# Head of a graph-transformer block: x in smaller pieces on two queues, edge lists cast by ScalarE, rows and columns in another order

## The chip, the cores and the metric

The kernel runs on one core of a Trainium2 chip. Its time is the device time of one execution in microseconds; the figure used is the median of several runs. A core has five engines that work side by side, each on its own list of instructions: TensorE (PE, with its weight loads PEld), VectorE (DVE), ScalarE (ACT), GpSimd (POOL) and SyncE (SP, which only issues transfers and synchronises). Transfers are issued from the queues of SP, ScalarE and GpSimd; the engine that issues one spends a few tenths of a microsecond on it and goes on. An engine takes its instructions in order: where one waits, all behind it wait.

## The reference, cut to what matters

The inputs are x (625 rows of 768), two lists of 20625 edge ends, src and dst (sorted by dst), and many weights. The whole is one layer of a graph transformer:

```python
xn = _layernorm(x, axis=-1)
x = x + gnn(xn, stack([src, dst]), ...) + mix(xn[None], ...)[0]
x = x + ffn(_layernorm(x, axis=-1)[None], ...)[0]
```

`gnn` is a first dense layer x1 = relu(xn @ W_ah + b_ah), three graph attentions over x1 with four heads each, and an output product. `mix` is a linear attention with a projection. `ffn` is a softmax attention, a normalisation over all elements, and a mixture of eight experts of which two are used. For the head of the kernel only this counts: xn is the normalised x; x1 is computed from xn; and the edges have to be turned into a 625 by 625 matrix of counts, how many edges go from each source to each target.

## The kernel before, in words

The 625 rows of x are five blocks of 125 rows, one row per partition. `xs` holds them. The head does the following.

- **Loads** (L141 to L162, an order written out by hand for SP and ScalarE): src goes out on ScalarE's queue and dst on SP's; then blocks 0 and 1 of x, by `load_x` and `move_rows` (L73): 112 rows in one transfer and the remaining 13 in a second. Block 0 is on SP, block 1 on ScalarE. Then SP issues the first half of W_ah (`wah0`, 1152 KB) and blocks 2 to 4; ScalarE issues `brow0`, the bias of the first dense layer. Outside that hand-written order, ScalarE has `fetch` (L189), a one-column copy ahead of which the activation table is loaded.
- **Are the edges near their place?** dst is sorted, so the target of edge number e is near a straight line. VectorE subtracts the line (L216), takes the absolute value (L217), the largest per partition (L219) and compares it with a bound (L220); a one-column matmul into the bank `psfar` adds the partitions up (L222), and `missed` (L224) becomes 0 or 1. All engines read `missed` at L262 and skip a slow path where it is 0.
- **Edge columns.** src and dst arrive as 55 partitions of 375. VectorE casts them from integer to float (`rf`, L226), TensorE transposes them, three pieces each, into the banks `ps_0` and `ps_1` (L231), and VectorE copies the banks to `src_f` and `dst_f` (L235), from which the 0/1 matrices for the counting products are made later (L249, L255).
- **First rows.** `row_stats` takes mean and variance of a block (two statistics instructions L88, one aggregation L90, an addition L92, all VectorE) and raises the variance to the power of minus one half on GpSimd (`rs`, L94). `norm_rows` writes the normalised block `xn` on VectorE (L207). `first_rows` (L319) transposes it on TensorE, four pieces into one bank and two into another (`ptx`, L323); ScalarE copies the banks to `xnT` (L324).
- **First products.** With `xnT` of blocks 0 and 1 TensorE begins x1 (`psx`, L357) in `x1_slice`; ScalarE applies bias and relu (L368).

The accumulator banks psfar, ps_0, ps_1, pb0 (the transposed bias, L497), ptx and psx are of one pool with four banks (`psb`, L109); one that its last reader has left goes to the next tile that asks.

Order of the work: in this part VectorE, TensorE and GpSimd follow the order of the program text (`manual_schedule` at L212, L213 and L495), ScalarE is in the text's order for the loads alone. What is not written out so is ordered by a planner, which puts instructions that it takes to be ready by their place in the text. Semaphores are inserted by the compiler.

Of the kernel before, what the change touches and what calls it, by code (L numbers as in the profile page):

```python
# [11 lines left out]
I32 = mybir.dt.int32  # L12
U32 = mybir.dt.uint32
AF = mybir.ActivationFunctionType
OP = mybir.AluOpType
# [7 lines left out]
TP = 125  # L23
# [16 lines left out]
def kernel(ctx: ExitStack, tc: tile.TileContext, a: dict, out: bass.AP):  # L40
    nc = tc.nc
# [31 lines left out]
    def move_rows(engine, dst, src):  # L73

        engine.dma_start(dst[0:112], src[0:112])
        engine.dma_start(dst[112:TP], src[112:TP])
# [7 lines left out]
    def row_stats(src, name):  # L84

        st = small.tile([TP, 2, 6], F32, tag="st", name=f"st_{name}")
        for j in range(2):
            nc.vector.bn_stats(st[:, j, :], src[:, j * HALF:(j + 1) * HALF])  # L88
        mv = small.tile([TP, 2], F32, tag="mv", name=f"mv_{name}")
        nc.vector.bn_aggr(mv, st.rearrange("p a b -> p (a b)"))  # L90
        ve = small.tile([TP, 1], F32, tag="ve", name=f"ve_{name}")
        nc.vector.tensor_scalar_add(ve, mv[:, 1:2], 1e-5)  # L92
        rs = small.tile([TP, 1], F32, tag="rs", name=f"rs_{name}")
        nc.gpsimd.tensor_tensor(rs, ve, mhalf[0:TP, 0:1], OP.pow)  # L94
        return mv, rs
# [16 lines left out]
    def b1(name):  # L112
        return psb.tile([P, BANK], F32, tag="b1", name=name)

    def mm(name):
        return psm.tile([P, 2 * BANK], F32, tag="mm", name=name)
# [6 lines left out]
    apool = es.enter_context(tc.tile_pool(name="apool", bufs=1, reuse_waits="tile"))  # L123
# [13 lines left out]
    NJ3 = NJ // 3  # L137
    SPREAD = 20
    idx_i = []
# [4 lines left out]
        eng.dma_start(idx_i[s], a[name].rearrange("(q e) -> q e", q=NJ3))  # L144
    xs = xpool.tile([TP, NT, D], F32, name="xs")
    def load_x(t):
        move_rows(nc.scalar if t == 1 else nc.sync, xs[:, t, :], a["x"][t * TP:(t + 1) * TP, :])

    wah = {}

# [3 lines left out]
    for t in range(2):  # L154
        load_x(t)
    load_ah(0)
    for t in range(2, NT):
        load_x(t)
# [26 lines left out]
    ones_col = const.tile([P, 1], F32, name="ones_col")  # L185
# [18 lines left out]
    def norm_rows(t, stats=None):  # L204
        mv, rs = stats or row_stats(xs[:, t, :], f"x{t}")
        xn = ohp.tile([TP, D], F32, tag="xn", name=f"xn{t}", bufs=3)
        nc.vector.tensor_scalar(xn, xs[:, t, :], mv[:, 0:1], rs, op0=OP.subtract, op1=OP.mult)  # L207
        return xn
# [4 lines left out]
    with tc.manual_schedule(engines={mybir.EngineType.DVE}):  # L213

        rf = [mxp.tile([P, N], F32, tag="kk", name=f"rf{s}", bufs=2)[0:NJ3, 0:3 * TP] for s in range(2)]
        nc.vector.scalar_tensor_tensor(odd, odd, -0.5 * PER, idx_i[1], op0=OP.mult, op1=OP.add)  # L216
        nc.vector.scalar_tensor_tensor(odd, odd, -1.0, odd, op0=OP.mult, op1=OP.max)  # L217
        far_s = small.tile([NJ3, 1], F32, tag="fs", name="far_s")
        nc.vector.tensor_reduce(far_s, odd, AX.X, OP.max)  # L219
        nc.vector.tensor_scalar(far_s, far_s, float(SPREAD), None, op0=OP.is_gt)  # L220
        ps = b1("psfar")
        nc.tensor.matmul(ps[0:1, 0:1], far_s, ones_col[0:NJ3], start=True, stop=True)  # L222
        missed = apool.tile([1, 1], I32, name="missed")
        nc.vector.tensor_scalar(missed, ps[0:1, 0:1], 1.0, None, op0=OP.min)  # L224
        for s in range(2):
            nc.vector.tensor_copy(rf[s], idx_i[s])  # L226
        ps = []
        for s in range(2):
            ps.append(b1(f"ps_{s}"))
            for r in range(3):  # L230
                nc.tensor.transpose(ps[s][0:TP, r * NJ3:(r + 1) * NJ3], rf[s][:, r * TP:(r + 1) * TP], ident[0:NJ3, 0:NJ3])  # L231
        st = [row_stats(xs[:, t, :], f"x{t}") for t in range(2)]
        xn = [norm_rows(0, st[0])]
        for s, f in enumerate((src_f, dst_f)):
            nc.vector.tensor_copy(f.rearrange("p (q r) -> p r q", r=3), ps[s][0:TP, 0:NJ].rearrange("p (r q) -> p r q", r=3))  # L235
        xn.append(norm_rows(1, st[1]))

        nc.vector.scalar_tensor_tensor(far, far, -PER, dst_f, op0=OP.mult, op1=OP.add)
        nc.vector.tensor_scalar(far, far, -0.5 * PER, None, op0=OP.add)
        nc.vector.scalar_tensor_tensor(far, far, -1.0, far, op0=OP.mult, op1=OP.max)  # L240
        nc.vector.tensor_scalar(far, far, float(SPREAD), None, op0=OP.is_gt)
        dst_all = apool.tile([TP, NJ], F32, name="dst_all")
        nc.vector.tensor_copy(dst_all, dst_f)
        nc.vector.scalar_tensor_tensor(dst_f, far, -2.0 * N, dst_f, op0=OP.mult, op1=OP.add)
        xn.append(norm_rows(2))
# [17 lines left out]
    with tc.If(again, preferred_fallthrough_block=True, label="far"):  # L263
        nc.vector.tensor_scalar(far, far, 2.0 * N, -2.0 * N, op0=OP.mult, op1=OP.add)
        nc.vector.tensor_add(far, far, dst_all)
        with tc.For_i(0, NJ, 1) as i:
# [4 lines left out]
            for b in range(NT):  # L271
                ps = mm(f"far{b}")
# [286 lines left out]
    for t in range(NT):  # L559
        nc.vector.tensor_sub(r12[:, t, 0, :], adn[:, t, :], mx[:, t, :])  # L560
        nc.vector.scalar_tensor_tensor(r12[:, t, 1, :], adn[:, t, :], 0.2, mx[:, t, :],
                                       op0=OP.mult, op1=OP.subtract)
# [143 lines left out]
    for g in range(2):  # L706
        w = load_w(rows(a["L0_mix_w_proj"], g * HALF, (g + 1) * HALF), f"wproj{g}")
        for t in range(NT):
            ps = b1(f"pspr{g}_{t}")
            for k in range(NC):  # L710
                nc.tensor.matmul(ps[0:TP, 0:HALF], yT[:, k, t * TP:(t + 1) * TP], w[:, k, :],  # L711
                                 start=(k == 0), stop=(k == NC - 1))
# [3 lines left out]
    ps = mm("psrT")  # L716
# [346 lines left out]
    ps = b1("psrs")  # L1063
# [45 lines left out]
    for hv in range(2):  # L1109
        lo, hi = HV[hv]  # L1110
        for c in range(NC):
            g, cc = divmod(c, 3)
            ps = b1(f"psw2{hv}{c}")
            for k in range(NC):
                nc.tensor.matmul(ps[:, 0:hi - lo], w2[g][:, k, cc * P:(cc + 1) * P], o2T[:, k, lo:hi],  # L1115
                                 start=(k == 0), stop=(k == NC - 1))
# [42 lines left out]
    for c in range(NC):  # L1159
        if c in (2, 5):  # L1160
            nc.scalar.activation(x3[:, c, 0:N], hT[:, c, :], AF.Identity, bias=gbi[:, c:c + 1], scale=gsc[:, c:c + 1])
        else:
            nc.vector.tensor_scalar(x3[:, c, 0:N], hT[:, c, :], gsc[:, c:c + 1], gbi[:, c:c + 1],
                                    op0=OP.mult, op1=OP.add)
# [139 lines left out]
    for k in range(2):  # L1304
        prw = a["L0_ffn_proj_w"][bass.ds(ex[k], 1), :, :].rearrange("e (f p) c -> p (e f) c", p=P)
        for u0 in range(0, HF, GU):
            hb = []
            for f in range(u0, u0 + GU):
# [11 lines left out]
                t = [ep.tile([P, NH2], F32, tag=f"t{q}", name=f"t{q}_{k}_{f}", bufs=GU + 2) for q in (1, 2, 4)]  # L1320
# [3 lines left out]
            for c in range(3):  # L1324
# [6 lines left out]
                for q in range(4):  # L1331
                    cc = c + 3 * (q // 2)
                    lo, hi = (0, NH2) if q % 2 == 0 else (NH2, N)
# [27 lines left out]
    def half(g):  # L1361
        return slice(g * HALF, (g + 1) * HALF)
# [23 lines left out]
    for i, (t, g) in enumerate(early):  # L1386
        if i == 0:
            nc.vector.scalar_tensor_tensor(xs[:, t, half(g)], ln2w[0:TP, half(g)], ngm[0:TP], xs[:, t, half(g)],
                                           op0=OP.mult, op1=OP.add)
# [7 lines left out]
    for i, at in enumerate([next(w) for w in (e, l, l, e, l, l, e, l, l, e)]):  # L1397
        t, g = at
        ps, dst = banks[at][0:TP, 0:HALF], fin[:, t, half(g)]
# [37 lines left out]
```

## Time and profile before

| what | value |
|---|---|
| median of 3 runs | 1338.31 us (1337.48 to 1338.95) |
| profiled execution | 1337.78 us |
| its span | 1336.0 us |
| TensorE clock granted | 0.997 of full |
| TensorE busy | 1305.2 us, 98% |
| VectorE busy | 794.2 us, 59% |
| ScalarE busy | 269.1 us, 20% |
| transfers | 109.00 MB, 82 GB/s on average |
| start of the first psx product | 13.28 us |

All times inside an execution are counted from the start of the span. In a line of the timeline the first number is the start, the second the duration in us, then engine, line, operation, output and inputs with their shapes; the bracket gives the engine's idle time before it and what ended it. An engine with a q behind its name is that engine's queue at work, such as issuing a transfer. In a line of the chain there are start, duration and what ran. In a line of waits there are the total in us, the number of times and the longest.

### The profile page before, as it was taken

The page shows a single profiled execution, that of the slowest core. Times are in us where ns is not written, and L with a number is a line of the kernel's source. Part 1 is how long each engine was busy: PE and PEld are TensorE (multiplying, and loading weights), DVE is VectorE, ACT ScalarE, POOL GpSimd, SP SyncE. Part 2 cuts the span into 40 slices and gives each one's busy share as a digit, 9 for nine tenths or more (in the row PEclk, how much of TensorE's full clock was granted, in tenths as well). Part 3 has the DMA queues.
Part 4 walks back from the last instruction along what each step waited for, and adds up shares of the span by engine and source line. Part 5 has one row for each costly group of instructions (what it writes and reads, how often), then busy time and mean ns, then how long its engine had stood idle before and what let it go on. Part 6 is the DMA issues. An engine that isn't in the chain of part 4 may idle for free.

```text
span 1336.0 us, 15063 instructions
## 1 busy us (share of the span) xinstructions
PE 1305.2 (98%) x5341; PEld 919.1 (69%) x5341; DVE 794.2 (59%) x2043; ACT 269.1 (20%) x550; POOL 79.5 (6%) x139
## 2 busy tenths in 40 slices
PE   7999999999999999999999969999999999999998
PEld 6676677556777895555667747777777777777776
DVE  7789687847575674675553386435543454445444
ACT  2122122014566570001011013101210021002100
POOL 3000111100000000000001130000000000000001
PEclk9999999999999999999999989999999999999999
DMA  8453232422212331103214132222212221322111
GB/s 242 130 149 89 75 102 73 145 86 74 73 63 69 107 103 35 36 26 105 71 36 139 36 110 67 62 74 83 72 56 82 83 71 49 86 80 72 48 48 58
DMA packets 124288, 109.00 MB, mean 82 GB/s; under 512 B 8990, under 2 KB 116470, under 8 KB 124212
## 3 DMA queue, kind: packets, MB, share of 16 engines
q1 hardware_dynamic: 114746, 84.79, 21.3%
q0 software_dynamic: 8464, 21.81, 5.2%
q10 hardware_dynamic: 1002, 1.43, 0.4%
q8 instruction: 42, 0.69, 0.2%
q14 instruction: 34, 0.28, 0.1%
HBM read 104.03 MB, written 3.96 MB: 81 GB/s over the span
## 4 chain that ended last, share of the span: by engine, by line
PE 89%; DVE 4%; issue 3%; ACT 2%; DMA 1%; POOL 0%; SPq 0%; DVEq 0%; ACTq 0%; POOLq 0%
PE psq L357 7%; PE ga_f L1206 6%; PE de_f L1206 6%; PE al_p L1206 6%; PE de_p L1206 6%; PE ga_p L1206 6%; PE al_f L1206 6%; PE psg L672 5%; PE cnt L257 3%; PE m_o L767 3%; PE be_f L1206 3%; PE pspr L711 3%; PE psw L1115 3%; PE be_p L1206 3%; PE psx L357 3%
## 5 line engine op out<-in xcount | busy, mean ns | idle before, releaser
L357 PE MATMUL psq<-xnT,wqkv 128*128 128x313 f32 (+1 forms) x432 | 121.8, 431 | 0.0
L672 PE MATMUL psg<-h,pt 125*125 125x193 f32 x600 | 101.2, 327 | 0.4 <-ACT node L677 0.4
L672 PEld LDWEIGHTS psg<-h,pt 125*125 125x125 f32 x600 | 98.5, 188 | 4.2 <-ACT node L677 0.7
L357 PEld LDWEIGHTS psq<-xnT,wqkv 128*128 128x128 f32 x432 | 78.9, 189 | 29.2
L1206 PE MATMUL al_f<-x,wf 128*128 128x313 f32 x288 | 84.1, 426 | 3.0 <-DMA wf<-in_L_ffn_fc_w_dram 3.0
L1206 PE MATMUL de_f<-xt,wf 128*128 128x313 f32 x288 | 83.7, 426 | 0.0
L1206 PE MATMUL al_p<-h,wp 128*128 128x313 f32 x288 | 79.8, 427 | 0.0
L249 DVE TENSOR_SCALAR os<-iota,src_f 125x625 f16<-125x625 f16 x165 | 63.8, 386 | 20.9 <-PE cnt L257 20.9
L1319 ACT ACTIVATE h<-c_f,ec 128x313 f32<-128x313 f32 x72 | 40.1, 559 | 179.2 <-DVE c_f L1227 113.1
L1206 PEld LDWEIGHTS al_f<-x,wf 128*128 128x128 f32 x288 | 54.1, 189 | 24.9 <-issue 2.3
L1206 PEld LDWEIGHTS de_f<-xt,wf 128*128 128x128 f32 x288 | 54.5, 189 | 21.5
L1206 PEld LDWEIGHTS al_p<-h,wp 128*128 128x128 f32 x288 | 54.6, 190 | 21.0
L257 PE MATMUL cnt<-os,od 125*125 125x512 f16 (+1 forms) x418 | 66.4, 300 | 0.9 <-DVE od L255 0.8
L257 PEld LDWEIGHTS <-od 125*125 125x125 f16 x418 | 44.2, 137 | 25.1 <-DVE od L255 2.6
L653 DVE SCALAR_TENSOR_TENSOR pt<-rb,as,u 125x625 f32<-125x625 f32 x60 | 51.1, 865 | 14.7 <-ACT u L647 14.5
L255 DVE TENSOR_SCALAR od<-iota,dst_f 125x125 f16<-125x125 f16 x209 | 50.6, 255 | 15.2 <-PE cnt L257 14.7
L658 DVE SCALAR_TENSOR_TENSOR pt<-pt,AT 125x625 f32<-125x625 f32 x60 | 48.5, 808 | 8.7 <-ACT pt L656 8.4
L453 DVE CUSTOM_DVE_ANT_0 jm<-row,maskb 125x625 bf16<-125x625 f32 x60 | 48.8, 813 | 2.4 <-DMA row<-row_d 1.0
L647 ACT ACTIVATE u<-rb,asd 125x625 f32<-125x625 f32 x60 | 48.7, 814 | 0.8 <-DMA rb<-rT_d 0.7
L1206 PE MATMUL be_f<-xt,wf 128*128 128x313 f32 x144 | 43.8, 439 | 5.1 <-DVE wf L1193 5.1
L656 ACT ACTIVATE pt<-pt 125x625 f32<-125x625 f32 x60 | 43.5, 724 | 9.8 <-DVE pt L653 9.5
L346 DVE CUSTOM_DVE_ANT_0 jk<-wal,ab 128x192 f32<-128x192 f32 x144 | 41.8, 358 | 4.5 <-DMA ab<-in_L_gnn_a_dst_dram 2.0
(425 smaller groups left out, 2173.2 us busy)
## 6 DMA issues: line engine op xcount, KB each, us to landing
wf<-in_L_ffn_fc_w_dram SPq DMA_DIRECT2D x96, 192.0 KB
wp<-in_L_ffn_proj_w_dram SPq DMA_DIRECT2D x96, 192.0 KB
row<-row_d POOLq DMA_DIRECT2D x24, 305.2 KB, 3.7
rb<-rT_d POOLq DMA_DIRECT2D x12, 610.4 KB, 8.9
wal<-in_L_gnn_W_dram SPq DMA_DIRECT2D x18, 384.0 KB
wqkv<-in_L_mix_w_qkv_dram SPq DMA_DIRECT2D x18, 384.0 KB
wg<-in_L_gnn_W_dram SPq DMA_DIRECT2D x6, 1152.0 KB
wout<-in_L_gnn_W_out_dram SPq DMA_DIRECT2D x6, 1152.0 KB
```

Source lines behind the costliest of these rows:

```text
L249: nc.vector.tensor_scalar(os_, iota, src_f[:, j:j + 1], None, op0=OP.is_equal)
L255: nc.vector.tensor_scalar(od_, iota[:, b * TP:(b + 1) * TP], dst[:, j:j + 1], None, op0=OP.is_equal)
L257: nc.tensor.matmul(ps[0:TP, lo:hi], od_, os_[:, lo:hi], start=first, stop=last)
L346: nc.vector.tensor_tensor_reduce(jk, wal[n][:, h * GC:(h + 1) * GC], ab[l, s][:, h * GC:(h + 1) * GC], 1.0, 0.0, OP.mult, OP.add, wa[:, k, ...
L357: nc.tensor.matmul(ps[:, 0:hi - lo], w[:, k, c0:c0 + P], xnT[:, k, lo:hi], start=(k == 0), stop=(k == NC - 1))
L453: nc.vector.tensor_tensor_reduce(jk, row, maskb[:, i, :], 1.0, -3e38, OP.add, OP.max, mx[:, i, p:p + 1])
L647: nc.scalar.activation(u1, rb[:, 0, :], AF.Identity, bias=asd[:, t, p:p + 1])
L653: nc.vector.scalar_tensor_tensor(pt, rb[:, 1, :], as02[:, t, p:p + 1], u1, op0=OP.add, op1=OP.max)
L656: nc.scalar.activation(pt, pt, AF.Exp)
L658: nc.vector.scalar_tensor_tensor(pt, pt, 1.0, AT[:, t, :], op0=OP.min, op1=OP.mult)
L672: nc.tensor.matmul(ps[0:TP, 0:GC + 1], pts[s][:, i * TP:(i + 1) * TP], hs[u, s][0][:, hd, :], start=(s == 0), stop=(s == NT - 1))
L1206: nc.tensor.matmul(ps[:, 0:NH2], ws[k // 3][:, s, k % 3, :], b[blk](k), start=(first and k == 0), stop=(k == n - 1), skip_group_check=True)
```

## The change

Three things are done in the head; nothing after the first rows is touched.

1. Blocks 0 and 1 of x are each cut into three transfers: rows 0 to 63 on SP, rows 64 to 111 and 112 to 124 on ScalarE. Blocks 2 to 4 are as before.
2. The casts of src and dst (`rf`) are done by ScalarE. The matmul into `psfar` and `missed` come after the six transposes of the edge lists, in the text and so in TensorE's order; for VectorE `missed` is still ahead of the statistics.
3. Block 1 is normalised (`xn1`) before the copies to `src_f` and `dst_f`.

```diff
     def load_x(t):
-        move_rows(nc.scalar if t == 1 else nc.sync, xs[:, t, :], a["x"][t * TP:(t + 1) * TP, :])
+        rows_in = a["x"][t * TP:(t + 1) * TP, :]
+        if t > 1:
+            return move_rows(nc.sync, xs[:, t, :], rows_in)
+
+        for eng, lo, hi in ((nc.sync, 0, 64), (nc.scalar, 64, 112), (nc.scalar, 112, TP)):
+            eng.dma_start(xs[lo:hi, t, :], rows_in[lo:hi])
...
         rf = [mxp.tile([P, N], F32, tag="kk", name=f"rf{s}", bufs=2)[0:NJ3, 0:3 * TP] for s in range(2)]
+        for s in range(2):
+            nc.scalar.copy(rf[s], idx_i[s])
         nc.vector.scalar_tensor_tensor(odd, odd, -0.5 * PER, idx_i[1], op0=OP.mult, op1=OP.add)
         nc.vector.scalar_tensor_tensor(odd, odd, -1.0, odd, op0=OP.mult, op1=OP.max)
         far_s = small.tile([NJ3, 1], F32, tag="fs", name="far_s")
         nc.vector.tensor_reduce(far_s, odd, AX.X, OP.max)
         nc.vector.tensor_scalar(far_s, far_s, float(SPREAD), None, op0=OP.is_gt)
-        ps = b1("psfar")
-        nc.tensor.matmul(ps[0:1, 0:1], far_s, ones_col[0:NJ3], start=True, stop=True)
-        missed = apool.tile([1, 1], I32, name="missed")
-        nc.vector.tensor_scalar(missed, ps[0:1, 0:1], 1.0, None, op0=OP.min)
-        for s in range(2):
-            nc.vector.tensor_copy(rf[s], idx_i[s])
         ps = []
         for s in range(2):
             ps.append(b1(f"ps_{s}"))
             for r in range(3):
                 nc.tensor.transpose(ps[s][0:TP, r * NJ3:(r + 1) * NJ3], rf[s][:, r * TP:(r + 1) * TP], ident[0:NJ3, 0:NJ3])
+        ps_far = b1("psfar")
+        nc.tensor.matmul(ps_far[0:1, 0:1], far_s, ones_col[0:NJ3], start=True, stop=True)
+        missed = apool.tile([1, 1], I32, name="missed")
+        nc.vector.tensor_scalar(missed, ps_far[0:1, 0:1], 1.0, None, op0=OP.min)
         st = [row_stats(xs[:, t, :], f"x{t}") for t in range(2)]
         xn = [norm_rows(0, st[0])]
+        xn.append(norm_rows(1, st[1]))
         for s, f in enumerate((src_f, dst_f)):
             nc.vector.tensor_copy(f.rearrange("p (q r) -> p r q", r=3), ps[s][0:TP, 0:NJ].rearrange("p (r q) -> p r q", r=3))
-        xn.append(norm_rows(1, st[1]))
```

## The prediction

> **What bounds the kernel now.** I read the page's busy times first, then the waits of TensorE after 14 us, then the chain of waits from 0 us, then the timeline and the transfer waits of the first 24 us, where all edits lie.
>
> ```profile
> PE 1305.2 (98%) x5341; PEld 919.1 (69%) x5341; DVE 794.2 (59%) x2043; ACT 269.1 (20%) x550; POOL 79.5 (6%) x139
> PE be_f L1206 <- DVE wf L1193: 5.1, 1, 5.1
> PE psx L357 <- ACT xnT L324: 0.3, 1, 0.3
> ```
>
> TensorE is busy 98% of the span; its longest later waits, such as the 5.1 us before be_f, hang on results of the chain itself. From psx at 13.28 us to 60 us it never idles. So whatever moves psx moves the end one for one, and nothing else in the head counts.
>
> ```profile
> 1.68 5.02 DMA xs<-in_x_dram
> 6.80 1.03 DVE st_x L88 x2
> 9.62 0.60 DVE xn L207
> 10.27 2.36 PE ptx L323 x10
> 13.28 9.48 PE psx L357 x36
> ```
>
> That is the head's chain: the first rows of x land at 6.70, VectorE takes the statistics of both blocks (6.80 to 9.62), normalises block 0, TensorE transposes twelve times at 0.236 us, psx starts. What runs beside it:
>
> ```profile
> 2.29 0.32 ACTq L161 DMA_DIRECT2D brow<-in_L_gnn_b_ah_dram  x1
> 2.64 1.28 ACT L189 ACT_TABLE_LOAD   x1 [2.64 <-issue]
> 5.95 0.15 DVE L224 TENSOR_SCALAR missed<-psfar 1x1 int32<-1x1 f32 x1 [0.28 <-PE psfar L222]
> 6.02 0.33 DVE L226 CAST rf<-src_i 55x375 f32<-55x375 int32 x1
> 6.50 1.48 PE L231 MATMUL ps<-ident,rf 55*125 55x55 f32 x6 [0.59 <-DVE rf L226]
> 9.71 0.92 POOL L94 TENSOR_TENSOR rs_x<-ve_x,mhalf 125x1 f32<-125x1 f32 x1 [0.80 <-DVE ve_x L92]
> 10.13 0.38 DVE L235 COPY src_f<-ps 125x165 f32<-125x165 f32 x1
> 10.66 0.68 DVE L207 TENSOR_SCALAR xn<-xs,mv_x,rs_x 125x768 f32<-125x768 f32 x1
> SPq L75 <- DMA src_i<-in_src_dram: 1.4, 1, 1.4
> SPq L170 <- DMA wah<-in_L_gnn_W_ah_dram: 4.1, 2, 2.8
> ```
>
> VectorE is free only at 6.62, so the landing at 6.70 costs 0.1 to 0.2 us. The last two rows matter most. Counted over both issuing queues, x2's first piece is the 9th transfer and stands until 3.96 for the 1st, src_i; the first bias row of L170 is the 16th and waits for the 8th, wah0. A transfer waits on the issuing queue for the one eight places before it.
>
> **The change part by part.**
>
> *Casts moved.* VectorE loses two casts (6.02 to 6.62). On ScalarE a 375-column cast is not in the trace; its copies there take 0.37 us for 250 and 0.59 for 500 columns, so 0.48, the second starting some 0.43 later. Below: VectorE's 0.33; above: 0.8, the 125x625 ACTIVATE of L647. I take 0.48, the same kind of instruction.
>
> *What stands before them on ScalarE.* Its queue had src 0.63, two x pieces (0.33, 0.41), brow0 0.32. Now it has src, x0[64:112], x0[112:125], x1[64:112], x1[112:125], brow0, and only then the table load (1.28), fetch (0.19) and the casts. Two more issues alone are 0.33 + 0.41 and two gaps of 0.04: 0.82 us. And ten transfers come ahead of brow0 instead of six. With the queues alternating as before, the order is src, dst, x0[64:112], x0[0:64], x0[112:125], x1[0:64], x1[64:112], wah0, x1[112:125] (9th), x2 (10th), brow0 (11th). So x1[112:125] waits for src_i (3.96, as the row showed) and **brow0 waits for the third, x0[64:112]**. When does that land? In before each queue had 464 KB up to x0 and x1; twice that, 928 KB, summed over the windows (26, 198, 310, 295, then 219 GB/s per us from 1 us on) has moved at 5.45, and x0 landed 1.25 us later. x0[64:112] has 81 + 147 KB on its queue, twice is 456 KB, moved at 3.75: it lands near 5.0. Then brow0 issues 5.03 to 5.35, table load to 6.66, fetch to 6.87, rf 6.89 to 7.37, the second until 7.80.
>
> *The matmul of far_s and missed moved behind the transposes.* VectorE's order is written out, and `missed` (L224) still stands before the statistics of x0. It now waits for psfar, which stands behind six transposes that wait for the casts. Queued behind it: all statistics, xn, hence psx. Transposes 7.41 + 1.48 = 8.89; from psfar to missed 0.23 (5.72 to 5.95): 9.12; next instruction 0.07 later, plus 0.05 for waiting on a third piece: statistics start at **9.24 instead of 6.80, +2.44**.
>
> *Split of x0 and x1.* SP still issues four transfers up to wah0, with 472 KB ahead of it instead of 464: wah0 is as before. x0 has 552 KB ahead on both queues together, done at 4.06, landing 5.3. The Trainium skill speaks against it: "DMA: Bandwidth & Descriptors", Rules for kernel authors, says of two transfers to disjoint partition halves not to bother, as they share the same engines. The trace agrees that these are full (DMA share 0.92 to 1.08 from 3 to 6 us), but the order within the queues still brings block 0 forward. By the rule x0 lands at 6.7, by the rows at 5.3; against statistics that start at 9.24 both are worth nothing. The wait of `missed` hides it; in the rivals it has a price.
>
> *xn1 ahead of the copies.* xn0 moves to 11.98. xn1 waits for POOL's rs1, which took 0.92 instead of the 0.57 of rs0, ending only after xn0 was through: 9.71 + 2.44 + 0.92 = 13.07. So xn1 starts at 13.10 and src_f 0.59 later (as after xn0: 9.54 to 10.13), 13.69 to 14.07. In before the copies stood in the very gap that rs1 leaves. They free the banks ps_0 and ps_1. The pool has four (L109), given out in the order in which they come free: ptx0's first four transposes take psfar's, the fifth takes ps_0's and must wait for src_f. It starts at 14.11; in before at 10.27 + 4 x 0.236 = 11.21. **+2.90 us**, of which 0.46 is this edit. Were rs1 only 0.57, this edit would cost 0.1. Below zero it can't go: xn1 was in before ready (11.34) ahead of its turn on TensorE (11.68).
>
> *What is hidden.* x2's rows are needed at 22.77 and were normalised at 16.36; the later VectorE work moves by 3.0 against TensorE's 2.9. x4's last 13 rows are now the 16th transfer and wait for wah0 (10.7), so wah1 is issued near 12.1 instead of 9.05; it landed at 18.2 with the transfer engines full until 17.5 and is used at 25.3. brow0 is used by pb, long before ptx.
>
> *TensorE's clock.* psx took 624 ns each from 14.2 to 16.2 us and 374 from 17.2: half speed until 6.3 us after ptx began. Taken as that row, the half-speed stretch moves along and costs nothing more. The Trainium skill ("TensorE: Matmul & The Clock Gate", Part 1) says that the window which lifts it, 3.4 us, is free-running; then it ends between 3.4 and 6.8 us after the start, and at half cost the sum can move by up to 0.85 either way. I take 2.90 and keep this for the range.
>
> **Sum.** The profiled execution took 1337.78 (span 1336.0), so it becomes 1340.7; the median of the runs is 0.53 above it: 1338.31 + 2.90 = **1341.2 us, +0.22%**. A measurement of this kernel tells a change from none from about 0.2% on, which is 2.68 us (1335.63 to 1340.99): the forecast lies just beyond.
>
> **The rivals.**
> 1. *Not slower: ScalarE gets to its table load early.* fetch and the casts are not written into the order of the load block; the planner may put them ahead of the waiting pieces. Or the wait on the third transfer may not be there, and the six issues end at 3.43: casts until 5.85, missed 7.2, statistics 7.3; +0.5 + 0.46 = 1.0: 1339.3. With the table load ahead of the last pieces, 1338.9. It decides where the table load starts before 5.16 instead of 5.38. For it: nothing else on ScalarE is held. Against: in before the table load came behind brow0. Chance 0.18.
> 2. *brow0 ahead of x2 in the count.* It is then the 10th and waits for dst, landed at 3.8; it issues at 4.41: 0.62 less, 1340.6. Chance 0.07.
> 3. *The first ptx group takes ps_0's bank.* All twelve transposes wait for src_f: 14.11 - 10.27 = 3.84: 1342.1. Against it: psfar comes free first. Chance 0.08.
> 4. *The planner orders later stages differently.* Only a few places of TensorE's order depart from the program's, but TensorE's idle time is 31 us; a few lost waits of the size of the 5.1 us give 1343 to 1348. Chance 0.08.
> 5. *Faster, as the parts alone promise.* If `missed` held nothing, statistics could start at 5.75, 1.05 earlier: at most 1337.3, within 0.2%; only a luckier order later gives 1335. Chance 0.05.
>
> **How the numbers follow.** The main case keeps 0.54; with cast, landing and clock its own range is 1340.3 to 1342.3, and some 0.63 of it lies above 1340.99. Slower: 0.34 + 0.01 + 0.08 + 0.08 = 0.51. Faster: 0.04. Same: 0.45. The range leaves out the fast end of rival 1, rival 5, and the far half of rival 4: 1338.2 to 1343.6.
>
> **What would show it.** Right: in the timeline after, brow0's issue near 5.0, the table load behind it, missed near 9.1 with its wait put down to psfar, statistics at 9.2, src_f after xn1, the fifth ptx behind src_f, psx near 16.2; x4's second piece waiting for wah. Wrong: a table load at 2.7 to 3.5, missed before 8, or psx before 15.3; or a TensorE wait after 60 us that was not there.

## The result, and the profile after

The changed kernel takes **1339.33 us** (median of 22 runs, 1336.81 to 1342.3); the kernel before, in 22 runs beside it, 1337.74 us (1334.84 to 1338.95). The ratio taken over these runs is 1.0019, with a 95% interval from 1.0013 to 1.0025: slower by 0.19%, some 2.5 us. (The two medians are 1.59 us apart, the two means 2.32; single runs of one kernel spread over 4 to 5.5 us, so the loss is known to about a microsecond.) The profiled execution took 1339.11 us, its span 1337.3 us, against 1337.78 and 1336.0 before.

The busy times of the page and TensorE's later waits:

```profile
PE 1307.4 (98%) x5341; PEld 920.2 (69%) x5341; DVE 793.6 (59%) x2041; ACT 269.3 (20%) x552; POOL 77.5 (6%) x139
```

```profile
PE be_f L1211 <- DVE wf L1198: 4.4, 1, 4.4
PE al_f L1211 <- DMA wf<-in_L_ffn_fc_w_dram: 0.8, 1, 0.8
```

The second of these was longer before:

```profile
PE al_f L1206 <- DMA wf<-in_L_ffn_fc_w_dram: 3.0, 2, 1.8
```

Nothing has changed in kind: TensorE is the bound and VectorE has lost two casts. After 14 us no wait of TensorE is there that was not there before; be_f waited 4.4 us instead of 5.1, al_f 0.8 instead of 3.0. What the change can have made worse lies in the head. The chain of waits there (start, duration, what ran):

```profile
0.82 2.88 DMA src_i<-in_src_dram
...
3.73 6.05 DMA xs<-in_x_dram
...
9.80 1.03 DVE st_x L88 x2
...
11.33 0.93 POOL rs_x L94
...
12.29 0.68 DVE xn L212
12.96 0.30 DVE src_f L241
...
15.55 8.88 PE psx L362 x36
```

Before, this chain began with the first rows of x and ran through both statistics. Now it begins with src: a transfer of x goes out at 3.73, when src has landed at 3.70, and itself takes 6.05 us. It is the last 13 rows of block 1. Behind it stand block 1's statistics, `rs` of block 1, xn1, the copy of src_f, and the transposes that wait for that copy. psx begins at 15.55 instead of 13.28, **2.27 us later**.

The timeline of the same stretch, in the order of the prediction's steps:

```profile
1.48 2.57 ACTq L152 DMA_DIRECT2D xs<-in_x_dram  x4
...
4.08 0.30 ACTq L166 DMA_DIRECT2D brow<-in_L_gnn_b_ah_dram  x1
4.10 0.54 DVE L223 SCALAR_TENSOR_TENSOR odd<-odd,dst_i 55x375 f32<-55x375 f32 x1 [0.98 <-DMA dst_i<-in_dst_dram]
...
4.42 1.28 ACT L194 ACT_TABLE_LOAD   x1 [4.42 <-DMA xs<-in_x_dram]
4.45 0.33 SPq L75 DMA_DIRECT2D xs<-in_x_dram  x1
...
5.35 0.69 SPq L76 DMA_DIRECT2D xs<-in_x_dram  x1
...
5.81 0.50 ACT L222 CAST rf<-src_i 55x375 f32<-55x375 int32 x1
...
6.08 0.44 SPq L75 DMA_DIRECT2D xs<-in_x_dram  x1
...
7.62 0.31 SPq L76 DMA_DIRECT2D xs<-in_x_dram  x1
...
8.07 0.15 DVE L236 TENSOR_SCALAR missed<-psfar 1x1 int32<-1x1 f32 x1 [2.11 <-PE psfar L234]
8.18 1.02 DVE L88 BATCH_NORM_STATS2 st_x<-xs 125x6 f32<-125x384 f32 x2
...
9.80 1.02 DVE L88 BATCH_NORM_STATS2 st_x<-xs 125x6 f32<-125x384 f32 x2 [0.17 <-DMA xs<-in_x_dram]
...
13.40 1.90 PE L328 MATMUL ptx<-ident,xn 125*128 125x125 f32 x8 [0.41 <-DVE src_f L241]
```

(The bracket of the table load names a transfer, but the load begins 0.04 us after brow0's issue ends, at 4.38: it is the next on its engine.)

Two limbs meet at the statistics of block 1. One is the limb of the prediction: brow0, table load, casts, transposes, `missed` at 8.07 after a wait of 2.11, statistics of block 0 at 8.18. By itself it would let those of block 1 begin at 9.63. The other is the landing of the 13 rows: they begin at 9.80, after 0.17 of waiting. The bracket is small, but it is small because the other limb is nearly as long.

The SP rows tell when the earlier pieces landed, if a transfer waits for the one eight places before it, as the prediction read it from before. x2's first piece (4.45) is the 11th transfer and waits for x0[64:112]; the 12th (5.35) for x0[0:64], the 13th (6.08, without a wait of its own) for x0[112:125], the 14th (7.62) for x1[0:64]. So block 0 was complete between 5.35 and 6.08, against 6.70 before, and of block 1 the first 64 rows were there by 7.62. Its 13 rows came at 9.78.

### The profile page after: what moved, and what is told of

Same layout as the page of the kernel before. It is cut to its first block, busy times and chain, and to the rows that moved or that the text cites. A ratio compares the mean times of both kernels' runs of the same rounds, so it can differ in the third digit from the quotient of the medians.

```text
span 1337.3 us, 15067 instructions
## 1 busy us (share of the span) xinstructions
PE 1307.4 (98%) x5341; PEld 920.2 (69%) x5341; DVE 793.6 (59%) x2041; ACT 269.3 (20%) x552; POOL 77.5 (6%) x139
## 4 chain that ended last, share of the span: by engine, by line
PE 89%; DVE 4%; issue 3%; ACT 2%; DMA 2%; POOL 0%; DVEq 0%; ACTq 0%; POOLq 0%
PE psq L362 6%; PE de_f L1211 6%; PE ga_f L1211 6%; PE al_p L1211 6%; PE de_p L1211 6%; PE ga_p L1211 6%; PE al_f L1211 6%; PE psg L677 5%; PE cnt L262 3%; PE m_o L772 3%; PE be_f L1211 3%; PE pspr L716 3%; PE psw L1120 3%; PE be_p L1211 3%; PE psx L362 3%
```

## The experiments

The **recorded theory** (B in the expectations) is the prediction's chain: `missed` behind the late casts holds VectorE, plus the order of xn1 and the copies; the split itself is hidden. The **rival** (A) was formed from the profile after: the last piece of block 1, as ninth transfer, lands near 9.8, and that alone holds the head. In all kernels but the first three, the rest of the change stays in. None leaves anything of the work out. Each ratio is against the kernel before, run beside it (its median lay between 1335.45 and 1337.74 us in these series, so times of different experiments should not be subtracted); the brackets hold the 95% interval. Starts and waits are from one profiled execution each.

**The split alone**, on the kernel before.

```diff
-        move_rows(nc.scalar if t == 1 else nc.sync, xs[:, t, :], a["x"][t * TP:(t + 1) * TP, :])
+        rows_in = a["x"][t * TP:(t + 1) * TP, :]
+        if t > 1:
+            return move_rows(nc.sync, xs[:, t, :], rows_in)
+
+        for eng, lo, hi in ((nc.sync, 0, 64), (nc.scalar, 64, 112), (nc.scalar, 112, TP)):
+            eng.dma_start(xs[lo:hi, t, :], rows_in[lo:hi])
```

> The kernel before with the split of x0 and x1 alone. Theory A (the last 13 rows of x1, now the 9th transfer, wait for src_i and land near 9.8 us): statistics of x0 start near 6.7, those of x1 near 9.8 instead of 8.17, xn0 near 11.2, psx near 14.9 instead of 13.28: +1.6 us. Theory B (only the wait of missed behind the casts and the order of xn1 cost time; the split is hidden or brings x0 forward): statistics of x1 near 8.1, psx 13.2 to 13.3: no change.

1338.72 us (16 runs), ratio 1.0023 [1.0015, 1.0031]: as slow as the whole change. Its timeline:

```profile
9.88 1.02 DVE L88 BATCH_NORM_STATS2 st_x<-xs 125x6 f32<-125x384 f32 x2 [1.75 <-DMA xs<-in_x_dram]
```

The casts are VectorE's here, block 0's statistics begin at 6.71, and then VectorE stands 1.75 us for the 13 rows. psx begins at 14.99, 1.71 us later than before, all of it from this wait. That the split is hidden is refuted.

**The casts and `missed` alone**, with the old loads and the old order of xn1.

```diff
+        for s in range(2):
+            nc.scalar.copy(rf[s], idx_i[s])
...
-        for s in range(2):
-            nc.vector.tensor_copy(rf[s], idx_i[s])
```

(The matmul into psfar and `missed` stand behind the transposes, as in the change.)

> The kernel before with the casts on ScalarE and psfar and missed behind the transposes, but x loaded as before and the copies ahead of xn1. The table load is then at 2.64 again, casts 4.2 to 5.1, transposes 4.7 to 6.2, missed near 6.4. Theory A: statistics of x0 at 6.75, bound by the landing of x0, psx 13.2, no change. Theory B as on record (casts on ScalarE make missed late by themselves, whatever the transfers): missed not before 7.2, psx 13.7 or later, +0.5.

1336.05 us (12 runs), ratio 0.9994 [0.9986, 1.0003]: no difference. Its timeline:

```profile
2.62 1.28 ACT L189 ACT_TABLE_LOAD   x1 [2.62 <-issue]
...
4.01 0.50 ACT L217 CAST rf<-src_i 55x375 f32<-55x375 int32 x1
...
6.47 0.14 DVE L231 TENSOR_SCALAR missed<-psfar 1x1 int32<-1x1 f32 x1 [0.28 <-PE psfar L229]
...
7.05 1.02 DVE L88 BATCH_NORM_STATS2 st_x<-xs 125x6 f32<-125x384 f32 x2 [0.44 <-DMA xs<-in_x_dram]
```

With brow0 early the table is loaded at 2.62, the casts end at 4.92, and `missed` waits for its own chain on VectorE (far_s), not for them. The statistics then waited for x0, which in this execution landed 0.25 us later than in that of before.

**The order of xn1 and the copies alone.**

```diff
         xn = [norm_rows(0, st[0])]
+        xn.append(norm_rows(1, st[1]))
         for s, f in enumerate((src_f, dst_f)):
             nc.vector.tensor_copy(...)
-        xn.append(norm_rows(1, st[1]))
```

> The kernel before with xn1 ahead of the copies to src_f and dst_f alone. Both theories: xn1 stays at 10.66 (bound by rs1), src_f moves from 10.13 to about 11.25 and ends at 11.65, the fifth ptx waits for it from 11.21: psx +0.45, at 13.7. Against it: the fifth ptx gets a bank that is free, psx stays at 13.28.

1336.66 us (12 runs), ratio 1.0006 [0.9998, 1.0015]. Its timeline:

```profile
10.20 0.67 DVE L207 TENSOR_SCALAR xn<-xs,mv_x,rs_x 125x768 f32<-125x768 f32 x1
...
11.31 0.68 DVE L207 TENSOR_SCALAR xn<-xs,mv_x,rs_x 125x768 f32<-125x768 f32 x1 [0.44 <-POOL rs_x L94]
11.90 0.37 DVE L236 COPY src_f<-ps 125x165 f32<-125x165 f32 x1
...
12.33 1.93 PE L323 MATMUL ptx<-ident,xn 125*128 125x125 f32 x8 [0.31 <-DVE src_f L236]
...
14.52 9.81 PE L357 MATMUL psx<-xnT,wah 128*128 128x250 f32 x36 [0.25 <-ACT xnT L324]
```

VectorE idles 0.44 us for block 1's `rs`, the gap in which the copies stood before; the fifth transpose waits for src_f. From xn0 to psx it is 4.32 us instead of 3.74, so the mechanism costs **0.58 us**. In the run's time that is too little to be told from nothing.

**`missed` taken out of the way**, in the changed kernel: it stands between the two statistics, so that the casts can't hold block 0's.

```diff
+        st = [row_stats(xs[:, 0, :], "x0")]
         nc.vector.tensor_scalar(missed, ps_far[0:1, 0:1], 1.0, None, op0=OP.min)
-        st = [row_stats(xs[:, t, :], f"x{t}") for t in range(2)]
+        st.append(row_stats(xs[:, 1, :], "x1"))
```

> The changed kernel with missed between the statistics of x0 and those of x1. Theory A: statistics of x0 start near 6.1 instead of 8.18, but those of x1 still at 9.8, psx stays at 15.4 to 15.55. Theory B (missed is what holds the head): everything comes forward by the wait of missed, 2.1 us, psx 13.5 to 14.

1338.2 us (20 runs), ratio 1.0016 [1.0009, 1.0023]: still slower. Its timeline:

```profile
5.83 1.02 DVE L88 BATCH_NORM_STATS2 st_x<-xs 125x6 f32<-125x384 f32 x2
...
10.41 1.02 DVE L88 BATCH_NORM_STATS2 st_x<-xs 125x6 f32<-125x384 f32 x2 [2.24 <-DMA xs<-in_x_dram]
```

Block 0's statistics begin at 5.83 without a wait, 2.35 us earlier than in the changed kernel, and nothing is gained: VectorE waits 2.24 us for the 13 rows, which came 0.6 us later here than in the other execution.

**The 13 rows earlier.** Two ways: one transfer on ScalarE brings rows 112 to 124 of both blocks, so that nothing of blocks 0 and 1 is the ninth; or block 1's 13 rows go to SP's queue, ahead of wah0.

```diff
-        for eng, lo, hi in ((nc.sync, 0, 64), (nc.scalar, 64, 112), (nc.scalar, 112, TP)):
-            eng.dma_start(xs[lo:hi, t, :], rows_in[lo:hi])
+        nc.sync.dma_start(xs[0:64, t, :], rows_in[0:64])
+        nc.scalar.dma_start(xs[64:112, t, :], rows_in[64:112])
+        if t == 0:
+            nc.scalar.dma_start(xs[112:TP, 0:2, :], a["x"][0:2 * TP].rearrange("(u p) d -> p u d", p=TP)[112:TP])
```

> The changed kernel with the last 13 rows of x0 and x1 in one transfer, so that all of x0 and x1 are within the first eight transfers and only brow0 is the 9th. Theory A: x1 lands before 8, the table load is near 4.1, missed near 7.7, statistics of x0 7.85, of x1 9.25, psx near 15.0, 0.55 less than the changed kernel. Theory B: missed alone, the same 0.3 to 0.4 less. If psx stays at 15.5, the late landing of x1 doesn't come from its place as 9th transfer.

1337.07 us (12 runs), ratio 1.0007 [0.9998, 1.0015]. Its timeline:

```profile
7.63 0.15 DVE L238 TENSOR_SCALAR missed<-psfar 1x1 int32<-1x1 f32 x1 [1.73 <-PE psfar L236]
...
9.12 1.02 DVE L88 BATCH_NORM_STATS2 st_x<-xs 125x6 f32<-125x384 f32 x2
```

```diff
-(nc.scalar, 112, TP)
+(nc.sync if t else nc.scalar, 112, TP)
```

> The changed kernel with the last 13 rows of x1 issued by SP, right behind x1's first 64 rows and ahead of wah0. The pieces have the same shapes, but this one is now the 8th transfer and waits for none; brow0 is the 9th and wah0 the 10th. If its late landing (9.78 us in the changed kernel) comes from its being the 9th transfer, issued near 3.7: statistics of x1 start at VectorE's own time, near 9.3, missed near 7.8, psx near 15.1. If the shape or the number of pieces makes it late: statistics of x1 again at 9.8 or later.

1337.01 us (15 runs), ratio 1.0012 [1.0005, 1.002]. Its timeline:

```profile
3.57 0.28 ACTq L166 DMA_DIRECT2D brow<-in_L_gnn_b_ah_dram  x1
3.84 0.41 SPq L66 DMA_DIRECT2D wah<-in_L_gnn_W_ah_dram  x1
...
9.05 1.02 DVE L88 BATCH_NORM_STATS2 st_x<-xs 125x6 f32<-125x384 f32 x2
```

In both, block 1's statistics have no wait for a transfer any more. But they begin at 9.12 and 9.05, not at the 8.17 of before: now the recorded theory's limb is the longer one (`missed` waits 1.73 for psfar). With the order's 0.6 psx begins at 14.87 and 14.79, 1.59 and 1.51 us later than before. So A, that the 13 rows alone hold the head, is too strong as well: by the start of psx, **each limb keeps most of the delay when the other is taken away.** In time, the first way can't be told from no change, the second is slower by 0.05 to 0.2%. (The second way also delays wah0, the price of the place it took on SP. And the order of the two issues, brow0 at 3.57 and wah0 at 3.84, is of use below.)

**Is it the shape of the 13-row piece?** Block 1's three transfers in reverse order: 13 rows early, 48 rows last, in ninth place.

```diff
-for eng, lo, hi in ((nc.sync, 0, 64), (nc.scalar, 64, 112), (nc.scalar, 112, TP)):
+for eng, lo, hi in ((nc.sync, 0, 64), (nc.scalar, 64, 112), (nc.scalar, 112, TP))[::-1 if t else 1]:
```

> The changed kernel with the 13 last rows of x1 issued ahead of its rows 64 to 111, so that the 9th transfer is the one of 48 rows. If a transfer issued behind the wait lands late whatever its shape: statistics of x1 again near 9.8 or later, psx 15.5. If it is the 13-row shape that lands late: statistics of x1 at 9.6, bound by VectorE, psx 15.35.

One execution, 1338.21 us.

```profile
10.95 1.02 DVE L88 BATCH_NORM_STATS2 st_x<-xs 125x6 f32<-125x384 f32 x2 [1.35 <-DMA xs<-in_x_dram]
```

The piece in ninth place is the late one, whichever rows it holds. In this one execution, then, it is the place, not the shape; what it is about the place is taken up in the last section.

**The order undone in the changed kernel**: the copies again ahead of xn1.

> The changed kernel with the copies to src_f and dst_f ahead of xn1 again. Both theories: the copies fall into the gap while GpSimd works on rs1 (11.8 to 12.3), the fifth ptx doesn't wait (0.41 us now), psx near 15.1 instead of 15.55, -0.45. Against it: no change.

1338.09 us (12 runs), ratio 1.0009 [1.0001, 1.0018]. Its timeline:

```profile
10.76 1.02 DVE L88 BATCH_NORM_STATS2 st_x<-xs 125x6 f32<-125x384 f32 x2 [1.11 <-DMA xs<-in_x_dram]
...
12.85 2.76 PE L328 MATMUL ptx<-ident,xn 125*128 125x125 f32 x12 [2.46 <-DVE xn L212]
```

All twelve transposes run in one piece again, and from xn0 (12.13) to psx (15.87) it is 3.74 us, as before. psx is nonetheless later than in the changed kernel, since the 13 rows landed at 10.7 in this execution. The interval overlaps that of the change, so the run's time doesn't show the 0.6 by itself.

**A version without either limb.** Blocks 0 and 1 in four transfers instead of six (block 0 as 64, 48 and the joint 13-row piece, block 1's first 112 rows in one on SP), `missed` between the statistics, copies ahead of xn1. With src, dst, wah0 and brow0 these are eight.

> A version for the gain: x0 split over both queues, its last 13 rows with those of x1 in one transfer, x1's other 112 rows on SP, so that src, dst, x0, x1, wah0 and brow0 are the first eight transfers and none waits; casts on ScalarE; missed between the statistics of x0 and x1; copies ahead of xn1. Theory A: statistics of x0 near 5.75, of x1 7.1, xn0 8.5, psx near 12.2, 1.1 us less than the kernel before and 3.3 less than the changed one. Theory B: missed near 7.1 or later holds x1's statistics, psx 12.4 or later. If splitting two halves over two queues brings nothing, x0 lands at 6.7 and psx is 13.2.

1336.58 us (13 runs), ratio 1.0003 [0.9994, 1.0012].

```profile
6.20 1.02 DVE L88 BATCH_NORM_STATS2 st_x<-xs 125x6 f32<-125x384 f32 x2 [0.28 <-DMA xs<-in_x_dram]
...
14.17 1.02 DVE L88 BATCH_NORM_STATS2 st_x<-xs 125x6 f32<-125x384 f32 x2 [1.70 <-DMA xs<-in_x_dram]
...
25.01 0.83 PE L332 MATMUL ptx<-ident,xn 125*128 125x125 f32 x6 [1.75 <-DVE xn L215]
```

psx begins at 12.75, 0.53 us earlier than before, the first version with a gain there. Now block 2 is late (VectorE waits 1.70 us for it at 14.17), and TensorE, which never waited here before, waits 1.75 us for a block's xn at 25.01. The gain is given back: the next group of psx begins at 25.94 instead of 25.34.

To take that wait away, GpSimd's five copies into A were moved ahead of the two `rs`, out of the way of the later ones.

> The version with eight first transfers (e7_eight) with GpSimd's five copies of the identity into A moved ahead of rs, into its idle time before 7.7 us. In e7_eight they stood between rs2 and rs3, and the normalised block 4 came 1.75 us too late for TensorE. If that wait gave back the gain: psx at 12.75, no wait of ptx for xn4 near 25 us, 1.5 to 2 us less than e7_eight, 1 to 1.5 less than the kernel before. If block 4 is late by its transfer: the wait stays.

1335.7 us (13 runs), ratio 0.9999 [0.9991, 1.0008].

```profile
3.73 1.53 POOL L240 COPY A<-ident 125x125 f32<-125x125 f32 x5
...
23.80 0.83 PE L331 MATMUL ptx<-ident,xn 125*128 125x125 f32 x6 [0.45 <-DVE xn L215]
```

The wait shrinks to 0.45 us, psx begins 0.36 us earlier than before and the next group 0.61 us (24.73), and the time is the same as before; a gain of 1 to 1.5 us, as expected, is not there, and 0.6 us would be lost in the interval. None of these versions beats the kernel before by what can be measured.

All together, from one profiled execution each (starts in us):

| kernel | statistics, block 1 | psx | psx against before | psx stretch | ratio of runs |
|---|---|---|---|---|---|
| before | 8.17 | 13.28 | | 9.48 | |
| the change | 9.80 | 15.55 | +2.27 | 8.88 | 1.0019 |
| split alone | 9.88 | 14.99 | +1.71 | 9.02 | 1.0023 |
| casts alone | 8.43 | 13.53 | +0.25 | 8.12 | 0.9994 |
| order alone | 8.83 | 14.52 | +1.24 | 9.81 | 1.0006 |
| `missed` later | 10.41 | 16.16 | +2.88 | 8.84 | 1.0016 |
| one 13-row piece | 9.12 | 14.87 | +1.59 | 8.78 | 1.0007 |
| 13 rows on SP | 9.05 | 14.79 | +1.51 | 9.83 | 1.0012 |
| 48 rows last | 10.95 | 16.70 | +3.42 | 9.62 | (one run) |
| copies first | 10.76 | 15.87 | +2.59 | 9.53 | 1.0009 |
| eight transfers | 7.63 | 12.75 | -0.53 | 8.69 | 1.0003 |
| the same, A copied early | 7.83 | 12.92 | -0.36 | 8.61 | 0.9999 |

Of the 1.24 of the order alone, 0.66 is that x0 landed later in that execution, though its loads are those of before. Both limbs come from the split: with the old loads (casts alone) the table is loaded at 2.62 and `missed` doesn't wait for the casts.

## Why the prediction was right, and where not

Direction and size held: +0.19% measured (1.0013 to 1.0025), +0.22% forecast; psx +2.27 us in the profile, +2.90 forecast. The bound, TensorE and the start of psx, was read rightly. That psx moves the end one for one holds only roughly, as far as the runs can tell: copies first has +2.59 us and 1.0009, the split alone +1.71 and 1.0023. The sum of the profile is 1.63 us up to xn0 and 0.64 from there to psx; the forecast had 2.44 and 0.46.

That the size came out is partly luck. The step that made most of it was 0.98 us too long, and a term put at nothing costs about the whole by itself; since the two meet at the same instruction they don't add, and the total stays near the forecast. Of the marks that the prediction set for being right, the links came true (src_f behind xn1, the fifth transpose behind src_f, `missed` waiting for psfar, x4 for wah0), but not the times: brow0 at 4.08 instead of near 5.0, `missed` at 8.07 instead of 9.1, psx at 15.55 instead of 16.2. `missed` and psx lie just on this side of its marks for being wrong, 8 and 15.3, and the table load is ahead of 5.16, the mark of the first rival.

- **Failed: "both are worth nothing. The wait of `missed` hides it."** The split was priced only by the landing of block 0, which it does bring forward. The step said that x1[112:125] is the ninth transfer and waits for src_i, and never asked when it lands. It lands at 9.78, and the wait for it ends the head in the changed kernel. The split alone costs as much as the whole change (1.0023 [1.0015, 1.0031]); the predicted mechanism came second, by 0.17 us.
- **Failed: "brow0 waits for the third, x0[64:112]."** It is the tenth, ahead of x2, and issued at 4.08 instead of 5.03, while the 11th, x2, stood until 4.45. 4.08 is also about when dst has landed, for which the tenth would wait (dst's reader on VectorE began at 4.10), and when the queue is done with the piece before; these aren't told apart here. With the 13 rows on SP the tenth is wah0, and it did stand for dst (the line below). That was the second rival. It took 0.95 us from the limb: table load 4.42 instead of 5.38, `missed` 8.07 instead of 9.12, statistics 8.18 instead of 9.24.

```profile
SPq L66 <- DMA dst_i<-in_dst_dram: 0.7, 1, 0.7
```

- **So the first limb was too long and the second was missing.** By the first alone the statistics of block 1 would have come 1.46 us later than before (9.63 against 8.17) instead of 2.44; the 13 rows added 0.17, and the order 0.18 more than forecast. These three, -0.98, +0.17 and +0.18, are the 0.63 by which psx came earlier than forecast. In three other executions with that piece in ninth place its reader began 0.1 to 1.0 us later than in this one, so the second limb is probably the longer one in most executions of the changed kernel too; that is argued, not shown.
- **Held: the casts' cost and the links behind them.** A cast takes 0.50 us, 0.48 was forecast; the second begins 0.40 after the first, 0.43 forecast. `missed` did wait for psfar, put down to it, with all statistics behind it. That this limb costs by itself is shown by the kernels without the late piece: 9.12 and 9.05 against 8.17.
- **Held: the order of xn1 and the copies**, mechanism and sign: src_f behind xn1, the fifth transpose behind src_f, `rs` of block 1 at 0.92. It measured 0.58 (alone) and 0.64 (in the change) instead of 0.46. Counted from xn0 to the fifth transpose, with the prediction's 11.21 for it in before, it is 0.46 alone and 0.56 in the change; the 0.12 and 0.08 that come behind are not explained.
- **Held: what was called hidden behind psx.** In the waits of SP's queue the second piece of x4 stands for wah0, as forecast (until 12.13, forecast 10.7):

```profile
SPq L76 <- DMA wah<-in_L_gnn_W_ah_dram: 3.8, 1, 3.8
```

  wah1 is issued at 13.41 (12.1 forecast), and no matmul waits for it.
- **The rule weighed against the rows.** "DMA: Bandwidth & Descriptors" of the Trainium skill (Rules for kernel authors) advises against splitting a transfer over disjoint partitions. By it block 0 would land at 6.7, by the rows at 5.3; it was complete between 5.35 and 6.08, and statistics began at 5.83 without a wait where `missed` didn't hold them. The order of the queues does count for when a block lands, then, as the prediction argued. That block 1 must pay for it, because the engines are shared, is not shown: with eight transfers first, block 0's statistics begin at 6.20 and block 1's at 7.63, both earlier than before, and it is block 2 that comes late. In the time of the kernel the advice holds: no kernel with the split was measurably faster than the one before (1.0023 to 0.9999).
- **The clock.** The psx stretch was 0.60 us shorter than before. Over the kernels above it lies between 8.12 and 9.83, without relation to its start; the margin of 0.85 either way was about right. The difference is how long its matmuls are slow: with casts alone they take 374 ns each from 14.5 us on, 4.0 us after the transposes began; with the 13 rows on SP 624 ns until 18.5, 7.4 us after, beyond the 6.8 that the prediction worked out as the latest. (From 624 to 374 is a factor of 1.67, not the two of its "half speed".) The rows of the granted clock show 1.00 in both.
- **Two single spans can't be subtracted.** Of psx +2.27 only 1.3 us are left between the two profiled spans. The stretch gives back 0.60. The other 0.3 is the balance of larger differences that go both ways: from 30 us on TensorE idles 19.2 us instead of 22.2, while its busy time over the whole span is 2.2 us longer. Over the twelve profiled executions that idle time lies between 16.0 and 22.2 us (be_f's wait alone between 1.8 and 6.4), more than the whole effect of the head.
- The rivals on the bank of ps_0 and on a planner's other order later did not occur: the first four transposes began at 11.90, ahead of the copies, and TensorE's waits after 14 us are at the same places as before.

## What to carry to other kernels

When a load is cut into more pieces, number all transfers of all queues in their order of issue, and price two things: when the last piece that somebody needs is issued and landed, and which instruction stands behind each issue on its engine. Here a small piece issued behind a large load on the other queue came late, so what is needed first is better issued ahead of it. A gain in the first block is worth nothing if its partner waits for a piece with a later number. And before moving an instruction ahead of another one, see whether the other stood in a gap that the moved one must wait out anyway.

## What the runs showed of the hardware that was not expected

- **A small transfer issued behind a large one on the other queue can stand for microseconds.** 13 rows (39 KB) issued at 3.73 landed at 9.78, 6.05 us later. In other executions with that piece in ninth place its reader began at 9.88, 10.41 and 10.76; with 48 rows there, at 10.95. brow0, 3 KB, issued at 4.08, was what the matmul on it still waited for at 9.36. The count of packets by queue (packets, MB, share of the 16 DMA engines' time) shows where the time went. q1 is SP's queue and q10 ScalarE's, by what each moved. The changed kernel from 6.5 to 7.8 us, and q10 from 7.8 to 9.2:

```profile
q1 hardware_dynamic: 311, 0.48, 105.4%
q10 hardware_dynamic: 1, 0.00, 0.0%
...
q10 hardware_dynamic: 38, 0.04, 9.9%
```

  So the 13 rows and brow0, all issued by 4.4, did not move at all before 7.8; meanwhile SP's queue moved its own, with wah0 (1152 KB), issued at 2.56, ahead of them. The two kernels with the 13 rows earlier separate the place from this. In both brow0 is the ninth, issued at 3.67 and 3.57; but in the first wah0 is issued ahead of it (2.56), in the second behind it (3.84). q10 of the first from 7.8 to 9.2, then of the second from 5.5 to 6.5 and from 6.5 to 9.2:

```profile
q10 hardware_dynamic: 12, 0.00, 1.1%
...
q10 hardware_dynamic: 31, 0.02, 11.5%
q10 hardware_dynamic: 1, 0.00, 0.0%
```

  Behind wah0, the queue's last packets, brow0's among them, moved after 7.8; ahead of wah0, all had moved by 6.5. That speaks for wah0, and against the ninth place or the wait as such, from one execution each. Why the queues are served in this order is open: with 48 rows last, ScalarE's queue moved 6 packets from 5.2 to 7.8 us, while SP's took only 84% of the engines' time.
- **The landing of the same load varies.** x0's statistics, released by the landing of x0 with the loads of before, began at 6.80, 7.05 and 7.45 in three executions. A single profile can't tell differences in the head of less than some 0.6 us by a starting time alone (of 1 us, where the piece in ninth place is waited for); the distances between instructions of one chain (3.74 from xn0 to psx in four kernels, 4.32 to 4.38 with xn1 first) are far steadier.
